# Local attention: the next row's preparation begins in the last step of the row ahead, turns of rotated rows stand later, output projections end blocks

## The chip, the cores and the metric

The kernel runs as one program on one core of a Trainium2 chip. The metric is the time of one launch on the device, in microseconds; the time of a kernel is the median of its runs. The engines are named as the profile names them: PE is TensorE (matrix products), PEld its weight loads, DVE is VectorE, ACT is ScalarE, POOL is GpSimd, SP is SyncE, which issues most transfers. Each engine takes its instructions from a queue of its own in a fixed order, and semaphores make it wait for the others.

## The reference, cut to what matters

The kernel computes a decoder of two layers on 8 rows of 512 tokens with 256 channels. The change lies in one part of it, the local attention, which occurs twice (once in each layer of a small local transformer). For each row it is:

```python
def _layer(x, wqkv, qs, ksc, wo, ...):
    h = shift_token(x)                 # half of the channels one token later
    qkv = h @ wqkv                     # 256 -> 3 * 512, 8 heads of 64
    q, k, v = jnp.split(qkv, 3, axis=-1)
    ...
    q = l2norm(q) * qs
    k = l2norm(k) * ksc
    q, k = rotary_xpos(q, k)           # cos, sin and a scale by position
    o = local_attention(q, k, v)       # windows of 128: own and previous one
    x = x + o @ wo                     # 512 -> 256
    ...                                # then a gated feed-forward on x
```

In `local_attention` a window of 128 queries sees the keys of its own window (causally) and of the one before; the softmax is over those.

## The kernel before, in words

The fast path (`FastDecoder`, `fast_stages`) runs self attention, cross attention, local attention 0, feed-forward 0, local attention 1, feed-forward 1, a quantized attention, a media attention and a mixture of experts. A stage is a Python generator that begins some of its work inside the stage ahead of it (`Ahead`); the local attention takes its row 0 through `prepare(0)` in that way.

**One row's preparation** (`prepare`, L1947) is cut into calls, which lie on eight slots of the row ahead of it:

- `turn(b, k)` (L1863): four transposes of the input's tiles into a bank, copied to `la_hT` by ScalarE.
- `project(b, i, j)` (L1882): tile i of 128 tokens (four tiles) times one third j of the weights: j = 0 and 1 are queries and keys, which ScalarE squares (`la_sq`, L1896) and copies (`la_qk`, L1897), j = 2 is the values, copied to `la_v` (L1894).
- `square` (L1901) and `root` (L1909): on VectorE, sums of squares by head and their inverse roots, for two tiles together.
- `rotate` (L1916): on VectorE, a scaling by the roots (L1920), two halves of the sine term (L1928, L1929), the cosine term (L1930) and an addition (L1931), on 128 x 1024 values.
- `turn_heads(b, i)` (L1933): eight transposes of the rotated tile in two banks of four, each copied to `la_qkT` by ScalarE (L1942).

**One row's attention** goes over four pairs of heads; a turn of the main loop (`for pair in range(0, n + 2, 2)`) takes one pair of heads and two slots. `scores(n)` (L1997) multiplies keys and queries into two PSUM tiles of two banks each, VectorE adds the mask (L2016) and ScalarE takes the exponential (L2020). `weigh(n)` (L2032) runs one pair later: values times weights into the bank `po`, copied to `la_o` by ScalarE (L2044); for each second pair also the denominators (`sum`), copied by VectorE (L2055). These go through DRAM (`inverted`, `times_rows`): two transfers, a reciprocal (L3306), one transfer, four broadcasts to `x_wide`, and then GpSimd multiplies (L3320) into `la_oT`. The last part is `project_out(b, i)` (L2067): four products for a tile of 128 tokens, added to the row by VectorE (L2076).

**Banks.** `turn`, `project`, `turn_heads` and `project_out` all take their PSUM bank from `self.pj()`, which has two buffers in turn. A group of products in a `pj` bank can start only when the reader of the group two before it is done.

**What sets the order.** The program's calls are laid out on the queues by a scheduler that takes priorities: what is made under `high_priority(self.AT_ONCE)` and in `together(n)` goes ahead, and `in_turn()` puts a call after the newest instruction of TensorE. `Background` (`later`) is a heap of calls with due times in ticks; each slot ticks it once and each call of a preparation once more. The output projections of a row come out of that heap, at 9, 12, 15 and 18 ticks after the last division:

```python
                    if c == 3:
                        for i in range(NST):
                            later.add(9 + 3 * i, lambda i=i: project_out(b, i))
```

The slots in the kernel before, with p = `project`, r = `rotate`, s = `square`, t = `turn_heads`: 0: both turns, p00, p01 and s0; 1: p10, p11, s1, root; 2: p20, r0, p21; 3: p30, r1, p31; 4: p02, s2, then t0, s3, root; 5: p12, r2, t1; 6: p22, r3, t2; 7: p32, t3.

Of the kernel before, what the change touches and what calls it, by code (L numbers as in the profile page):

```python
# [27 lines left out]
F32 = mybir.dt.float32  # L28
# [11 lines left out]
P = 128  # L40
# [1237 lines left out]
class FastDecoder(Decoder):  # L1278
# [557 lines left out]
    def local_attention(self, l, y, ahead):  # L1836
# [26 lines left out]
        def turn(b, k):  # L1863

            d = held.setdefault(b, {})
            if k == 0:
                d["hT"] = self.alloc(first, [P, 2, S], F32, "la_hT", bufs=1)
                d["v"] = self.alloc((first, second)[b % 2], [P, NST, S], F32, f"la_v{b % 2}", bufs=1)
                d["qkT"] = self.alloc((first, second)[b % 2], [P, 8, S], F32, f"la_qkT{b % 2}", bufs=1)
            hT = d["hT"]  # L1870
            ps = self.pj()
            for i in range(NST):
                nc.tensor.transpose(
                    ps[:, i * P : (i + 1) * P], y[:, b * NST + i, k * P : (k + 1) * P], self.ident
                )
            if k == 0:
                nc.scalar.copy(hT[:, 0, :], ps)
            else:
                nc.gpsimd.memset(hT[:, 1, 0:1], 0.0)
                nc.scalar.copy(hT[:, 1, 1:], ps[:, : S - 1])  # L1880

        def project(b, i, j):  # L1882
            d = held[b]
            if j == 0:
                d["rows", i] = self.alloc(first, [P, 2 * S], F32, "la_qk", bufs=4)
                d["sq"] = self.alloc(first, [P, 2 * S], F32, "la_sq")
            ps = self.pj()
            for k in range(2):
                nc.tensor.matmul(  # L1889
                    ps, d["hT"][:, k, i * P : (i + 1) * P], wqkv[:, k, j * S : (j + 1) * S],  # L1890
                    start=(k == 0), stop=(k == 1),
                )
            if j == 2:
                nc.scalar.copy(d["v"][:, i, :], ps)  # L1894
# [37 lines left out]

        def turn_heads(b, i):  # L1933
            d = held[b]
            for j in range(2):
                ps = self.pj()
                for c in range(4):
# [9 lines left out]
        def prepare(b):  # L1947

            def one(*calls):
# [8 lines left out]
                [one((p, 1, 0)), one((p, 1, 1), (s, 1), (root,))],  # L1958
                [one((p, 2, 0), (r, 0)), one((p, 2, 1))],
                [one((p, 3, 0), (r, 1)), one((p, 3, 1))],  # L1960
                [one((p, 0, 2), (s, 2)), one((t, 0), (s, 3), (root,))],
                [one((p, 1, 2), (r, 2)), one((t, 1))],
                [one((p, 2, 2), (r, 3)), one((t, 2))],
                [one((p, 3, 2)), one((t, 3))],
            ]

        second = None
# [7 lines left out]
        with self.tc.tile_pool(  # L1975
# [56 lines left out]
            def weigh(n):  # L2032
# [24 lines left out]
                def divide(rows):  # L2057
# [1 line left out]
                        oT = d["oT", c - 1 + j] = self.alloc(pool, [P, S], F32, "la_oT", bufs=6)  # L2059
                        self.times_rows(pool, oT, d["o", c - 1 + j], rows[2 * j : 2 * j + 2, :], later)  # L2060
                    if c == 3:
                        for i in range(NST):
                            later.add(9 + 3 * i, lambda i=i: project_out(b, i))

                self.inverted(pool, total[0:P:32, :], later, divide)

# [10 lines left out]

            n = 8 * B
            ahead.step()
            for pair in range(0, n + 2, 2):  # L2080
                if pair < n:
                    if pair % 8 == 0:
                        ready = prepare(pair // 8 + 1) if pair // 8 + 1 < B else [()] * 8
                    scores(pair // 2)
                if pair >= 2:
                    weigh(pair // 2 - 1)
                for i in (pair, pair + 1):
                    with self.in_turn():
                        later.tick(1)
                    if i < n:  # L2090
                        for thunk in ready[i % 8]:
                            with self.in_turn():
                                thunk()
                                later.tick(1)
                    if i == n - 6:
                        early.close()
                    if i > n - 6:
# [1 line left out]
                            ahead.step()  # L2099
            ahead.step(100)  # L2100
            later.drain()

    def local_ffn(self, l, y, ahead):

# [1472 lines left out]
```

## Time and profile before

| | us |
|---|---|
| median of 3 runs | 3036.18 (3035.45 to 3040.28) |
| the profiled execution, its own time | 3039.56 |
| its span, first to last instruction | 3037.8 |
| TensorE busy | 2832.6 |
| VectorE busy | 2039.3 |
| ScalarE busy | 1191.5 |
| GpSimd busy | 388.1 |
| local attention of layer 0, seven rows from 699.57 to 1087.59 | 388.0 |
| local attention of layer 1, seven rows from 1388.09 to 1773.18 | 385.1 |
| TensorE busy in these two stretches | 730.3 |

The page of the profile gives, for each group of instructions: the line of the kernel and the engine, what it writes and reads with the tiles' names, the number of instructions, their busy time and the mean of one in ns, and then the time that the engine sat idle just before them with the engine and line that ended it. A timeline gives the start and length of merged instructions, with the same idle time in brackets. The lengths of matrix products are modelled and overlap a little: a group that is followed at once by the next is listed some 0.15 us longer than the distance to the next start. The granted clock of TensorE over the whole execution is 0.972.

### The profile page before, as it was taken

To read this page: it belongs to the slowest core of one execution; us is meant where nothing else is said; L and a number is where in the kernel's file an instruction comes from. 1 tells how busy PE (TensorE), PEld (TensorE's weight loads), DVE (VectorE), ACT (ScalarE), POOL (GpSimd) and SP (SyncE) were. 2 spreads that over 40 slices of the span, in tenths; PEclk is the share of its full clock that TensorE was granted. 3 is DMA by queue.
4 is the path that set the end of the run, shared out by engine and by line. 5 is a ranking of instruction groups with operands and counts; after the bars stand their busy time and mean duration, and the time that the engine had idled before them with its cause. 6 is when DMAs were issued, how large, how long until landed. Compare 5 with 4: busy or idle time off the path is not lost. (4 is left out here: it accounts for less than half of the span.)

```text
span 3037.8 us, 39774 instructions
## 1 busy us (share of the span) xinstructions
PE 2832.6 (93%) x14929; PEld 1511.4 (50%) x14944; DVE 2039.3 (67%) x4546; ACT 1191.5 (39%) x1687; POOL 388.1 (13%) x357
## 2 busy tenths in 40 slices
PE   8999999979999999999999989998796999997998
PEld 5653333225555556555555556564444344444665
DVE  7458998977776784356776788548797766664110
ACT  2237776744444431124444431113364444441111
POOL 1111111100011110000101111101211012121111
PEclk9999999988999999999999999999897999997999
DMA  7011212101000011001000011001332132313331
GB/s 246 1 35 50 72 51 62 42 18 57 15 23 23 15 32 36 0 1 37 22 22 17 21 46 63 21 7 63 106 132 91 43 105 78 112 58 97 102 140 61
DMA packets 130694, 168.71 MB, mean 56 GB/s; under 512 B 51761, under 2 KB 79666, under 8 KB 128443
## 3 DMA queue, kind: packets, MB, share of 16 engines
q1 hardware_dynamic: 126394, 154.48, 16.3%
q0 software_dynamic: 4096, 11.59, 1.0%
q8 instruction: 119, 1.95, 0.3%
q14 instruction: 85, 0.69, 0.1%
HBM read 113.12 MB, written 47.50 MB: 53 GB/s over the span
## 5 line engine op out<-in xcount | busy, mean ns | idle before, releaser
L1889 PE MATMUL pj<-w,la_hT 128*128 128x512 f32 x720 | 334.2, 605 | 5.2 <-ACT la_qkT L1942 4.5
L1736 DVE TENSOR_TENSOR x_e<-x_e,x_share 128x1024 f32<-128x1024 f32 x256 | 315.9, 1277 | 14.3 <-ACT x_e L1735 14.1
L1735 ACT ACTIVATE x_e<-sc 128x1024 f32<-128x1024 f32 x256 | 249.2, 1023 | 83.8 <-PE sc L1724 83.8
L1889 PEld LDWEIGHTS pj<-w,la_hT 128*128 128x128 f32 x720 | 132.6, 191 | 153.4 <-issue 115.6
L2016 DVE TENSOR_TENSOR la_e<-sc,la_mask 128x1024 f32<-128x1024 f32 (+1 forms) x128 | 135.3, 1084 | 103.6 <-PE sc L2007 103.6
L3320 POOL TENSOR_TENSOR la_oT<-la_o,x_wide 128x512 f32<-128x512 f32 x64 | 97.7, 1538 | 753.1 <-DMA x_wide<-invs 678.6
L2945 ACT ACTIVATE ma_e<-sc,ma_bias 128x1024 f32<-128x1024 f32 x128 | 135.6, 1110 | 145.9 <-PE sc L2939 131.4
L2233 ACT ACTIVATE lf_gate<-pj,lf_b 128x512 f32<-128x512 f32 (+1 forms) x82 | 56.3, 687 | 333.3 <-PE pj L2212 318.0
L2020 ACT ACTIVATE la_e<-la_e 128x1024 f32<-128x1024 f32 (+1 forms) x128 | 117.5, 946 | 152.6 <-DVE la_e L2016 151.6
L2212 PE MATMUL pj<-lf_hnT,w 128*128 128x512 f32 (+1 forms) x368 | 171.4, 593 | 2.0 <-DVE lf_hid L2238 2.0
L1752 PE MATMUL po<-x_e,x_v 128*32 128x512 f32 x1024 | 140.7, 622 | 33.7 <-DVE x_e L1736 29.7
L2212 PE MATMUL sc<-lf_hnT,w 128*128 128x512 f32 x336 | 157.7, 592 | 0.0
L1724 PE MATMUL sc<-x_q,x_k 32*128 32x512 f32 x1024 | 152.9, 647 | 1.7 <-DVE sa_ok L1448 1.4
L2284 PE MATMUL po<-w,lf_hid 128*128 128x256 f32 x640 | 149.0, 379 | 0.0
L2238 DVE SCALAR_TENSOR_TENSOR lf_hid<-sc,lf_b,lf_gate 128x512 f32<-128x512 f32 x70 | 52.4, 749 | 136.4 <-PE sc L2212 133.4
L2027 PE MATMUL po<-la_e,la_v 128*64 128x256 f32 (+1 forms) x1024 | 125.8, 370 | 7.0 <-ACT la_o L2044 6.3
L2007 PE MATMUL sc<-la_qkT 64*128 64x256 f32 (+1 forms) x1024 | 128.9, 375 | 1.2 <-DVE la_e L2016 0.6
L2284 PEld LDWEIGHTS po<-w,lf_hid 128*128 128x128 f32 x640 | 117.8, 190 | 21.2 <-issue 7.4
L2939 PE MATMUL sc<-ma_qT,ma_kT 64*128 64x512 f32 x512 | 127.3, 615 | 0.4 <-ACT ma_e L2945 0.4
L2962 PE MATMUL po<-ma_e,ma_v 128*64 128x512 f32 x512 | 125.7, 612 | 0.0
L2070 PE MATMUL pj<-w,la_oT 128*128 128x256 f32 x512 | 121.0, 383 | 2.0 <-DVE lf_t L1480 0.7
L1905 DVE TENSOR_REDUCE la_ss<-la_sq 128x16 f32<-128x1024 f32 x64 | 77.7, 1215 | 65.8 <-ACT la_sq L1896 65.8
(500 smaller groups left out, 5173.6 us busy)
## 6 DMA issues: line engine op xcount, KB each, us to landing
x_wide<-invs SPq DMA_DIRECT2D x184, 128.0 KB
w<-in_f_w_dram SPq DMA_DIRECT2D x16, 1024.0 KB
kv<-kv_o SPq DMA_DIRECT2D x56, 256.0 KB
slots<-x_empty SPq DMA_DIRECT2D x8, 1028.0 KB
x_mask<-in_x_maskT_dram SPq DMA_DIRECT2D x8, 1024.0 KB
ma_kT<-kv SPq DMA_DIRECT2D x8, 1024.0 KB
ma_v<-kv SPq DMA_DIRECT2D x8, 1024.0 KB
ex_rows<-slots SPq DMA_DIRECT2D x7, 1028.0 KB
```

Of the source, the lines that this page charges most:

```text
L1724: nc.tensor.matmul(pair[r // 2][:, r % 2, :], d["k"][rows, g, kt * P : (kt + 1) * P], d["q"][rows, e, g, :], start=True, stop=True,)
L1735: nc.scalar.activation(ex, d["e"][rest][p], AF.Exp)
L1736: nc.vector.tensor_tensor(ex, ex, d["share"][:, kt, :].unsqueeze(1).broadcast_to([P, 2, 512]), ALU.mult)
L1752: nc.tensor.matmul(d["po"][32 * r : 32 * r + 32, :], d["v"][:, kt, 8 * g + 2 * r + e, :], ex[r // 2][:, r % 2, :], start=(kt == 0), stop=( ...
L1889: nc.tensor.matmul(ps, d["hT"][:, k, i * P : (i + 1) * P], wqkv[:, k, j * S : (j + 1) * S], start=(k == 0), stop=(k == 1),)
L2007: nc.tensor.matmul(both[half][:, r, jj * 256 : jj * 256 + to - j * P], d["qkT"][rows, 4 + c, j * P : (j + 1) * P], d["qkT"][rows, c, j * P ...
L2016: nc.vector.tensor_tensor(ex[:, :, :n_cols], ps[:, :, :n_cols], mask[:, :n_cols].unsqueeze(1).broadcast_to([P, 2, n_cols]), ALU.add,)
L2027: nc.tensor.matmul(out[:, j * P : to], lhsT(j), ex[:, jj * 256 : jj * 256 + to - j * P], start=(j == 0), stop=(j == 3), skip_group_check=True,
L2212: nc.tensor.matmul(ps[:m, :], w1[:, k, at : at + m], held[b]["hnT"][:, k, :], start=(k == 0), stop=(k == 1))
L2284: nc.tensor.matmul(ps[:, :C], held[b]["hid"][:, f, i * P : (i + 1) * P], w2[:, f, :], start=(f == 0), stop=False,)
L2939: nc.tensor.matmul(both[m // 2][:, r, :], d["k"][rows, c, kt * P : (kt + 1) * P], d["q"][rows, c, :], start=True, stop=True,)
L2945: nc.scalar.activation(ex, ps, AF.Exp, bias=bias[:, b * NST + kt : b * NST + kt + 1], scale=0.125)
```

## The change

Three things are moved in `local_attention`; the instructions of a row stay the same.

The preparation has nine lists in place of eight, and the first of them (both turns of the input, p00, p01, s0) is placed at the end of slot 7 of the row two before, so it lies behind t2 and t3 of the row one before. The others move up by one slot. The slots are now: 0: p10, p11, s1, root; 1: p20, r0, p21; 2: p30, r1, p31; 3: p02, s2, s3, root; 4: t0, p12, r2; 5: t1, p22, r3; 6: p32; 7: t2, t3, and then the first list of the next row. For row 1 the first list is put at the head of slot 0.

The output projections are no longer taken from the heap at fixed ticks. Two ticks after the last division they join a list `due`, and the end of each turn of the main loop takes from it 0, 1, 1 or 2 tiles by the pair's number; what is left is done after the stage.

The buffers of the values and of the turned heads are allocated at their first use rather than with the turned input.

```diff
@@ turn
             if k == 0:
                 d["hT"] = self.alloc(first, [P, 2, S], F32, "la_hT", bufs=1)
-                d["v"] = self.alloc((first, second)[b % 2], [P, NST, S], F32, f"la_v{b % 2}", bufs=1)
-                d["qkT"] = self.alloc((first, second)[b % 2], [P, 8, S], F32, f"la_qkT{b % 2}", bufs=1)
@@ project
             if j == 2:
+                if i == 0:
+                    d["v"] = self.alloc((first, second)[b % 2], [P, NST, S], F32, f"la_v{b % 2}", bufs=1)
                 nc.scalar.copy(d["v"][:, i, :], ps)
@@ turn_heads
+            if i == 0:
+                d["qkT"] = self.alloc((first, second)[b % 2], [P, 8, S], F32, f"la_qkT{b % 2}", bufs=1)
@@ prepare
                 [one((p, 1, 0)), one((p, 1, 1), (s, 1), (root,))],
                 [one((p, 2, 0), (r, 0)), one((p, 2, 1))],
                 [one((p, 3, 0), (r, 1)), one((p, 3, 1))],
-                [one((p, 0, 2), (s, 2)), one((t, 0), (s, 3), (root,))],
-                [one((p, 1, 2), (r, 2)), one((t, 1))],
-                [one((p, 2, 2), (r, 3)), one((t, 2))],
-                [one((p, 3, 2)), one((t, 3))],
+                [one((p, 0, 2), (s, 2), (s, 3), (root,))],
+                [one((t, 0)), one((p, 1, 2), (r, 2))],
+                [one((t, 1)), one((p, 2, 2), (r, 3))],
+                [one((p, 3, 2))],
+                [one((t, 2)), one((t, 3))],
@@ divide
                     if c == 3:
-                        for i in range(NST):
-                            later.add(9 + 3 * i, lambda i=i: project_out(b, i))
+                        later.add(2, lambda: due.extend((b, i) for i in range(NST)))
@@ main loop
+            due = []
+            coming = prepare(1)
+            first_calls = coming[0]
             for pair in range(0, n + 2, 2):
                 if pair < n:
                     if pair % 8 == 0:
-                        ready = prepare(pair // 8 + 1) if pair // 8 + 1 < B else [()] * 8
+                        b = pair // 8
+                        ready = list(coming[1:]) if b + 1 < B else [()] * 8
+                        coming = prepare(b + 2) if b + 2 < B else [()] * 9
+                        ready[7] = [*ready[7], *coming[0]]
+                        if b == 0:
+                            ready[0] = [*first_calls, *ready[0]]
...
+                for tile in due[: (0, 1, 1, 2)[pair // 2 % 4]]:
+                    with self.in_turn():
+                        project_out(*tile)
+                    due.remove(tile)
...
             later.drain()
+            for tile in due:
+                project_out(*tile)
```

More of the change, by code (lines that the diff above doesn't have):

```diff
@@ L2094, in local_attention @@
                                 later.tick(1)
+                for tile in due[: (0, 1, 1, 2)[pair // 2 % 4]]:
+                    with self.in_turn():
+                        project_out(*tile)
+                    due.remove(tile)
+                for i in (pair, pair + 1):
                     if i == n - 6:
```

## The prediction

> **What bounds the kernel now.** I read the busy table first, then the groups of instructions, then the stage itself as a timeline of each engine. The busy table says TensorE: 2832.6 us of 3037.8.
>
> ```profile
> PE 2832.6 (93%) x14929; PEld 1511.4 (50%) x14944; DVE 2039.3 (67%) x4546; ACT 1191.5 (39%) x1687; POOL 388.1 (13%) x357
> ```
>
> So only what TensorE waits for can be won. In the groups, one line of the two local-attention stages stands out:
>
> ```profile
> L1939 PE MATMUL pj<-ident,la_qk 128*128 128x128 f32 x480 | 77.6, 285 | 40.4 <-DVE x L2076 31.5 <-ACT la_qkT L1942 6.3 <-ACT la_v L1894 2.0
> ```
>
> The turns of rotated rows wait 40.4 us in all, 31.5 of it for the VectorE addition that empties an output projection's bank. One row of the first stage, on TensorE, shows where:
>
> ```profile
> 887.24 1.72 PE L2027 MATMUL sum<-la_e,ones 128*32 128x256 f32 x32
> 888.89 1.99 PE L2070 MATMUL pj<-w,la_oT 128*128 128x256 f32 x8
> 890.72 1.88 PE L1889 MATMUL pj<-w,la_hT 128*128 128x512 f32 x4
> 893.37 0.66 PE L1939 MATMUL pj<-ident,la_qk 128*128 128x128 f32 x4 [0.77 <-DVE x L2076]
> 893.95 1.79 PE L2007 MATMUL sc<-la_qkT 64*128 64x256 f32 x16
> 895.67 0.66 PE L1939 MATMUL pj<-ident,la_qk 128*128 128x128 f32 x4
> 896.16 1.89 PE L2070 MATMUL pj<-w,la_oT 128*128 128x256 f32 x8
> 897.89 1.88 PE L1889 MATMUL pj<-w,la_hT 128*128 128x512 f32 x4
> 900.82 0.66 PE L1939 MATMUL pj<-ident,la_qk 128*128 128x128 f32 x4 [1.05 <-DVE x L2076]
> ```
>
> Two banks named pj alternate over turns, projections and outputs, so each group waits for the reader of the group two before it. Here output, projection, turn: the turn needs the output's addition (0.33 us), which stands in VectorE's queue behind parts of a rotation of 1.2 us each. The third wait of the row is 0.70. Over the ten rows after the first two of each stage these three sum to 2.82 us a row on average (2.28 to 3.38), of some 55.4. [...] ScalarE's queue is in order, and what stands in it matters below:
>
> ```profile
> 899.00 1.79 ACT L2020 ACTIVATE la_e<-la_e 128x1024 f32<-128x1024 f32 x2 [2.05 <-DVE la_e L2016]
> 900.70 0.57 ACT L1894 COPY la_v<-pj 128x512 f32<-128x512 f32 x1
> ```
>
> The two exponentials wait for VectorE's mask additions, and the copy that frees a pj bank waits behind them. And a long wait has an aftermath; the turn that waits 2.79 is followed by weighing at 2.88 instead of 1.73, the one that waits 2.19 is not:
>
> ```profile
> 734.76 0.66 PE L1939 MATMUL pj<-ident,la_qk 128*128 128x128 f32 x4 [2.79 <-ACT la_qkT L1942]
> 735.35 2.88 PE L2027 MATMUL po<-la_e,la_v 128*64 128x256 f32 x16
> ...
> 1422.51 0.65 PE L1939 MATMUL pj<-ident,la_qk 128*128 128x128 f32 x4 [2.19 <-ACT la_qkT L1942]
> 1423.10 1.73 PE L2027 MATMUL po<-la_e,la_v 128*64 128x256 f32 x16
> ```
>
> **The change, part by part.** Nothing is added or taken away: per row 8 query/key projections, 4 value projections, 8 half turns, 4 outputs, 14 DMAs on SP. All is order. The built order of a middle row, counted from T, the end of the last denominators of the row before (865.16 in the row above), is now: half a turn of the input, projections 0 and 1 of tile 0, outputs 2 and 3, tiles 1 and 2, scores of pair 1, weighing, tile 3, value 0, output 0, scores 2, weighing, sums, turn 0 (two halves), scores 3, value 1, turn 1a, weighing, turn 1b, values 2, output 1, value 3, turns 2 and 3.
>
> *Taken away:* the three waits, 3.3 us a row. Outputs 2 and 3 stand at T+4 to T+7.5, where VectorE has only a reduction and a reciprocal ahead of their additions: the first is done at T+6.6, and tile 1 needs its bank at T+7.5. Output 0 has scores, weighing, sums and a half turn (5.5 us) between it and the group that needs its bank. No wait.
>
> *Put in its place, first: value 0.* From the row at 865 (start to start): projection 1.77, value 1.72, output 1.73, scores 1.71, weighing 1.67, sums 1.65, half turn 0.53. TensorE ends tile 1 at T+11.05, tile 2 at 14.6, scores 16.3, weighing 18.0, tile 3 at 21.5. VectorE starts the second reduction at 11.9 (1.13), then the root (2.72), two scalings (2.28), then the masks of pair 1 (2.0): 20.0. In ScalarE's order both exponentials (second one: 0.25 after its mask, 0.75), a copy of la_o (0.5), and only then square and copy of tile 3 (1.0): 22.5. Value 0 needs that bank: wait 1.0. In the kernel before, pair 1's masks came ahead of the reductions, so nothing waited here. GpSimd's two products lie over the root as before, where every other row lost 0.7 (turn 0 waits 0.77 in some rows, about 1.6 in others): +0.4 on average.
>
> *Second: turn 1b.* VectorE has no gap from T+20.0: two sine halves 1.20, reduction 1.13, cosine and addition 2.26, reduction 1.13, sine halves 1.20, output addition 0.33, cosine 1.13, 0.2, mask 1.0, addition 1.13, mask 1.0, rest of the root and the sums' copy 2.85, two scalings 2.28, masks of pair 3 2.0. Sum 18.9: T+38.9. Exponential, 0.25 later, 0.75; copy of value 1, 0.5; TensorE 0.14 later: 40.5. TensorE itself arrives: value 0 at 22.6, then 1.72+1.73+1.71+1.67+1.65+1.06+1.71+1.72+0.53+1.67 = 15.2: 37.8. Wait 2.7; a trace would show about 2.4 to 2.5[...]. Before, one scaling fewer stood ahead of these masks, and they ended at T+34.6.
>
> *Third:* turn 2 waits for output 1's addition (T+46.3) with TensorE there at 46.2: 0.2. The first projection waits 0.2 for its turned input, whose scores no longer stand between; the scores after turn 2 keep their 0.4 to 0.6.
>
> Per row: 1.0 + 0.4 + 2.7 + 0.2 + 0.2 = 4.5 against 3.3 and 0.3 of the interleaved scores' last wait, which goes: **+0.9**. Ten middle rows: +9.0. The first two rows of a stage, walked alike: the first waits at a turn as long as before (2.79 and 2.19 in the two stages), the second 2.1 at turn 1b where it had 1.6 to 1.7 twice with less after it; I take +0.3 a stage, +0.6.
>
> *The clock.* In this trace waits of 2.71, 2.79, 2.82 and 2.84 us were followed by matmuls at nearly double time, waits of 2.19 and 2.60 were not. One drop costs what the rows at 735 to 741 show: 1.14 on the weighing and 0.45 on the half turn, about 1.6. [...] By the rows it stands 0.25 short of the shortest wait that did[...]: ten rows, one drop taken, +1.6, bounds 0 and 10 x 1.6 = 16. I go by the rows: **+11.2**.
>
> *Edits at nothing.* The reciprocal of pairs 0 and 1 moves from T+36.1 to T+39.9; its DMAs and GpSimd's products follow 5.3 later (T+45.2). The la_o of pair 3 reuses pair 0's buffer (three buffers) and is copied at T+51.5, after the first product's end at 46.7: cover 5 us. The products now lie over the last rotation ahead of output 1's addition. The row for it: an addition of 1.22 took 1.97 at 907.73, with GpSimd busy. TensorE, already 2.7 late, has 0.6 to spare, so +0.1. [...] The later allocation of values and turned heads frees nothing that was waited for (value 0's buffer was last read before T). SP's queue keeps its order and count. The eight outputs of the last two rows stay behind the feed-forward's first chunk; the preparation of row 0 keeps its 18 calls. Nothing.
>
> Sum: 3039.56 (the profiled execution, span 3037.8) + 11.2; the median of the runs is 3.4 lower, 3036.18, so **3047**.
>
> **The rivals.** (a) *Faster:* turn 1b's wait is covered. It decides where pair 3's masks end: by T+36.3 instead of 38.9. Then value 1 is copied when TensorE arrives, the three old waits go (10 x 3.3), 1.4 + 0.4 stay: -1.8 x 10 = -18, 3018. For it: ScalarE is only 39% busy. Against: VectorE's 18.9 us hold no gap. (b) *No change:* turn 1b's wait is 1.8 us, as with VectorE 3% quicker than walked: +0 to +3, 3037. (c) *Clock in every row:* the wait crosses 2.7 in each: +9.6 + 16 to 28 (the drop at 1788.48 cost 2.8), 3062 to 3074.
>
> **How the numbers follow.** Likeliest, new waits with at most a few drops: 0.55 (3042.5 to 3054). (c) 0.15, (b) 0.18, (a) 0.12. The bound of 0.2% (6 us) is about what a measurement of this kernel can tell. Slower takes the likeliest case and (c), less a little of its lower edge: 0.69; same 0.19; faster 0.12. The range leaves half of (a) and half of (c) out: 3030 to 3065.
>
> **What would show it.** Right: turns no longer wait for the addition of x (31.5 us before); a half turn waits about 2.4 us for ScalarE's la_v in each middle row, value projections about 1 us for la_qk; TensorE's busy time unchanged; rows of about 56.3 us. Wrong: a half-turn wait under 1.5 us (VectorE's queue shorter than walked), or weighings of 2.9 us in each row (the clock).

## The result and the profile after

The changed kernel takes 3057.61 us (median of four runs, 3056.47 to 3061.03), the kernel before 3036.61 us beside it: 1.0071 times as long, 95% interval 1.0057 to 1.0085. The forecast was 3047. Its profiled span is 3059.3 us against 3037.8, so there are 21.5 us to find, where the sum had 11.2.

Two lines of the page and of the groups answer to those shown of before: TensorE's busy time, and the turns, with the projections beside them.

```profile
PE 2842.1 (93%) x14944; PEld 1518.6 (50%) x14944; DVE 2028.2 (66%) x4546; ACT 1184.8 (39%) x1687; POOL 383.5 (13%) x357
```

```profile
L1887 PE MATMUL pj<-w,la_hT 128*128 128x512 f32 x720 | 341.3, 614 | 19.5 <-ACT la_qk L1897 16.7 <-ACT la_qkT L1944 1.5 <-ACT la_hT L1875 0.7
L1941 PE MATMUL pj<-ident,la_qk 128*128 128x128 f32 x480 | 74.1, 288 | 40.1 <-ACT la_v L1894 31.7 <-DVE x L2078 5.8 <-ACT la_qkT L1944 2.0
```

The turns wait as long as before (40.1 against 40.4 us), but for somebody else: 31.7 us for ScalarE's copy of values where 31.5 us were for the addition of x. New are 16.7 us of the projections (5.2 in all before). TensorE is busy 9.5 us longer with the same products (15 of them, none in these stages, have no record in the trace of before); the projections alone went from 334.2 to 341.3. A row of the first stage, on TensorE, shows the new waits in their places:

```profile
883.16 3.70 PE L1887 MATMUL pj<-w,la_hT 128*128 128x512 f32 x8
888.55 1.98 PE L1887 MATMUL pj<-w,la_hT 128*128 128x512 f32 x4 [1.69 <-ACT la_qk L1897]
...
902.31 1.73 PE L2030 MATMUL po<-la_e,la_v 128*64 128x256 f32 x16
906.30 0.66 PE L1941 MATMUL pj<-ident,la_qk 128*128 128x128 f32 x4 [2.25 <-ACT la_v L1894]
...
910.33 1.88 PE L1887 MATMUL pj<-w,la_hT 128*128 128x512 f32 x4
912.76 0.66 PE L1941 MATMUL pj<-ident,la_qk 128*128 128x128 f32 x4 [0.55 <-DVE x L2078]
```

Value 0 waits 1.69 us for tile 3's copies, the second half turn of tile 1 waits 2.25 us, the turn of tile 2 waits 0.55. ScalarE's queue answers for the second in the same way as before:

```profile
903.99 1.79 ACT L2023 ACTIVATE la_e<-la_e 128x1024 f32<-128x1024 f32 x2 [4.31 <-DVE la_e L2019]
905.68 0.56 ACT L1894 COPY la_v<-pj 128x512 f32<-128x512 f32 x1
```

All this is as forecast. What the forecast walked, but didn't read as a limit of its own, is VectorE's timeline in that row. These are its first instruction behind a gap, the one after it, the masks of pair 3, the last two, and the next behind a gap:

```profile
877.08 1.22 DVE L1905 TENSOR_REDUCE la_ss<-la_sq 128x16 f32<-128x1024 f32 x1 [3.64 <-ACT la_sq L1896]
878.34 1.11 DVE L1913 TENSOR_SCALAR la_ss<-la_ss 128x32 f32<-128x32 f32 x1
...
902.74 2.08 DVE L2019 TENSOR_TENSOR la_e<-sc,la_mask 128x1024 f32<-128x1024 f32 x2
...
911.15 1.23 DVE L1931 TENSOR_TENSOR la_qk<-la_qk,la_r 128x1024 f32<-128x1024 f32 x1
912.30 0.41 DVE L2078 TENSOR_TENSOR x<-x,pj 128x256 f32<-128x256 f32 x1
914.84 1.23 DVE L2019 TENSOR_TENSOR la_e<-sc,la_mask 128x1024 f32<-128x1024 f32 x1 [2.14 <-PE sc L2010]
```

VectorE never stops from the squares of tile 1 to the addition that lets the turn of tile 2 begin: 35.6 us of a row of 57.9. In the kernel before the same stretch is there, with fewer instructions in it:

```profile
875.87 1.22 DVE L1905 TENSOR_REDUCE la_ss<-la_sq 128x16 f32<-128x1024 f32 x1 [2.38 <-ACT la_sq L1896]
877.12 0.43 DVE L1913 TENSOR_SCALAR la_ss<-la_ss 128x32 f32<-128x32 f32 x1
...
907.40 0.41 DVE L2076 TENSOR_TENSOR x<-x,pj 128x256 f32<-128x256 f32 x1
```

So a row can be read in another way, with T the end of the last denominators of the row before. Before: the stretch starts at T + 10.7, takes 31.9 us, and from the turn of tile 2 to the row's end TensorE needs 12.5: 55.1. After: it starts at T + 11.8, since two outputs stand ahead of tile 1, takes 35.6, and 10.45 follow: 57.9. Of the 3.7 us more, 3.5 are found: the masks of one pair of heads more (2.0), one last addition of a rotation more (1.15), 0.7 on a small instruction beside GpSimd's products (1.11 against 0.43), one output addition less (0.33). Two readings of one row, then: waits on TensorE that add up, or VectorE's stretch. The experiments tell them apart.

**The ledger of the 21.5 us**, from the starts and ends of rows in the two traces:

| stretch | before | after | difference |
|---|---|---|---|
| start of stage 0 (first scores) | 698.13 | 696.00 | -2.1 |
| first scores to the end of row 2, both stages | 111.2 + 108.5 | 108.2 + 101.8 | -9.7 |
| rows 3 to 6, eight in all | 222.4 + 221.6 | 235.3 + 232.2 | +23.5 |
| rows 7 and 8, both stages | 75.8 + 76.2 | 82.4 + 81.9 | +12.3 |
| end of stage 0 to start of stage 1 | 280.5 | 276.7 | -3.9 |
| behind stage 1 | 1243.3 | 1244.8 | +1.5 |

A middle row is 55.5 us before and 58.4 after. The first two rows end sooner and the last two later in part because work has changed places: in each stage row 2 holds two output projections where it held four, and row 7 six. Two of them take 3.5 us of TensorE.

### The profile page after: what moved, and what is told of

Read it like the earlier page. It is cut to its first block, busy times and chain, and to the rows that moved or that the text cites. A ratio compares the mean times of both kernels' runs of the same rounds, so it can differ in the third digit from the quotient of the medians.

```text
span 3059.3 us, 39825 instructions
## 1 busy us (share of the span) xinstructions
PE 2842.1 (93%) x14944; PEld 1518.6 (50%) x14944; DVE 2028.2 (66%) x4546; ACT 1184.8 (39%) x1687; POOL 383.5 (13%) x357
## 3 DMA queue, kind: packets, MB, share of 16 engines
q1 hardware_dynamic: 126394, 154.48, 16.2%
## 5 line engine op out<-in xcount | busy, mean ns | idle before, releaser
L1887 PE MATMUL pj<-w,la_hT 128*128 128x512 f32 x720 | 341.3, 614 | 19.5 <-ACT la_qk L1897 16.7
L2010 PEld LDWEIGHTS sc<-la_qkT 64*128 64x128 f32 x1024 | 93.8, 187 | 49.9 <-issue 20.4
```

What stands on the lines that cost most here:

```text
L1887: nc.tensor.matmul(ps, d["hT"][:, k, i * P : (i + 1) * P], wqkv[:, k, j * S : (j + 1) * S], start=(k == 0), stop=(k == 1),)
L2010: nc.tensor.matmul(both[half][:, r, jj * 256 : jj * 256 + to - j * P], d["qkT"][rows, 4 + c, j * P : (j + 1) * P], d["qkT"][rows, c, j * P ...
```

## The experiments

The theories: **1**, the recorded one, sums the waits on TensorE, so a wait that is taken away is paid back. **2**: VectorE's stretch sets when the turns of tiles 2 and 3 can come, and a wait ahead of them on TensorE only hides it. **3**: the clock, lowered behind waits. Each ratio is to the kernel before, run beside it on the same chip (3035.2 to 3039.4 us on the three chips of the experiments). The middle row is the mean of rows 3 to 6 of both stages, taken from each trace. The last column is the mean of those of the eight in which the profile shows a granted clock of 1.00 throughout, with their number: it leaves out what theory 3 is about.

| kernel | median us | ratio, 95% interval | middle row, us | at full clock, us (rows) |
|---|---|---|---|---|
| before | 3036.61 | 1 | 55.51 | 55.51 (8) |
| changed | 3057.61 | 1.0071 (1.0057 to 1.0085) | 58.44 | 57.84 (5) |
| changed, ScalarE's order | 3068.76 | 1.0100 (1.0078 to 1.0122) | 59.24 | 58.19 (3) |
| changed, VectorE's order | 3055.04 | 1.0052 (1.0032 to 1.0071) | 58.35 | 57.19 (2) |
| changed, both orders | 3034.11 | 0.9988 (0.9974 to 1.0003) | 55.96 | 55.96 (8) |
| changed, counts 2, 1, 1, 0 | 3054.59 | 1.0051 (1.0036 to 1.0065) | 58.26 | 57.56 (4) |
| counts, ScalarE's order | 3031.84 | 0.9984 (0.9975 to 0.9993) | 55.71 | 55.70 (8) |
| counts, both orders | 3025.10 | 0.9955 (0.9945 to 0.9965) | 55.35 | 55.35 (8) |
| counts, both orders, pair 1 | 3032.60 | 0.9985 (0.9976 to 0.9994) | 55.60 | 55.60 (8) |
| the same, output of block 1 held ahead | 3036.30 | 0.9993 (0.9983 to 1.0003) | 56.50 | 55.80 (3) |
| before, outputs at block ends | 3031.15 | 0.9971 (0.9960 to 0.9983) | 55.28 | 55.28 (8) |
| the same, ScalarE's order | 3037.99 | 1.0008 (0.9995 to 1.0022) | 55.61 | 55.08 (6) |
| changed without new grouping | 3044.11 | 1.0018 (1.0006 to 1.0031) | 56.54 | 56.54 (8) |
| changed without outputs at block ends | 3062.67 | 1.0078 (1.0052 to 1.0104) | 58.83 | 58.78 (5) |

### One order on ScalarE, one on VectorE, and both

The exponentials of pair 3 go behind the copy of value projection 1. TensorE, VectorE and GpSimd keep their orders.

```diff
-                nc.scalar.copy(d["v"][:, i, :], ps)
+                copied = nc.scalar.copy(d["v"][:, i, :], ps)
+                if i == 1:
+                    d["v1"] = copied.ins
...
-                    nc.scalar.activation(ex[:, :, :n_cols], ex[:, :, :n_cols], AF.Exp, scale=-1.0)
+                    with self.tc.issue_after(held[b + 1]["v1"]) if c == 3 and b + 1 < B else nullcontext():
+                        nc.scalar.activation(ex[:, :, :n_cols], ex[:, :, :n_cols], AF.Exp, scale=-1.0)
```

> The changed kernel with one order turned round on ScalarE: in each of the 14 rows that prepare another, the two exponentials of head pair 3 are issued behind the copy of the value projection of tile 1 instead of ahead of it (TensorE, VectorE and GpSimd keep their orders). Theory 1, the recorded one: the half turn of tile 1 waits 2.25 us for that copy and this wait is paid in full, so the kernel loses about 14 x 2.2 = 31 us: about 3027 us, and the half turn of tile 1 doesn't wait. Theory 2, VectorE's stretch: from the square reduction of tile 1 (877.08 in the row that starts at 865.29) to the addition ahead of the turn of tile 2 (912.71) VectorE has no gap, 35.6 us, and the wait at tile 1 only hides that the turn of tile 2 would come no sooner. Then the wait at tile 1 goes and the wait of the turn of tile 2 for the addition of x grows from 0.55 to about 2.8 us; the time stays within 4 us of 3057.6. Theory 3, the clock: the waits of 2.25 us lower the granted clock and cost by that; then about 7 us are gained, since projections took 341.3 us against 334.2 before.

Measured: 3068.76 us, slower than the changed kernel. TensorE in this kernel, in the same place of the same row:

```profile
899.51 1.73 PE L2033 MATMUL po<-la_e,la_v 128*64 128x256 f32 x16
901.17 0.66 PE L1943 MATMUL pj<-ident,la_qk 128*128 128x128 f32 x4
...
905.33 1.88 PE L1887 MATMUL pj<-w,la_hT 128*128 128x512 f32 x4
909.96 0.66 PE L1943 MATMUL pj<-ident,la_qk 128*128 128x128 f32 x4 [2.75 <-DVE x L2081]
```

The half turn of tile 1 (901.17) no longer waits. The turn of tile 2 does, 2.75 us for VectorE's addition instead of 0.55: the 2.25 us came back 5.9 us of work later, to within 0.05. Theory 1 falls here. Theory 2 has the wait right but not the time: the row of this excerpt is 57.9 us long, as in the changed kernel, others are up to 60.5. The idle time ahead of the local groups (the turns of the input left out) is the same in both profiles (71.7 and 71.2 us), while TensorE's busy time in them is 865.5 against 858.9. So part of what it lost, by the rows 0.45 of 0.80 us, is products run at a lower clock, in theory 3's way, behind the one wait of 2.75: in five of the eight middle rows the granted clock is 0.94 to 0.97, and these take 59.1 to 60.5 us; the other three take 57.9 to 58.6.

Next the other order alone: the addition that frees the bank goes ahead of the end of tile 3's rotation (ScalarE's order is that of the changed kernel).

```diff
-            nc.vector.tensor_tensor(q4, q4, cos, ALU.mult)
-            nc.vector.tensor_tensor(qk, qk, r, ALU.add)
+            if i == 3:
+                d["last"] = (qk, q4, cos, r)
+            else:
+                end_rotate(qk, q4, cos, r)
...
+        def end_last(b):
+            if adds:
+                with self.tc.issue_after(adds[-1]):
+                    end_rotate(*held[b]["last"])
+            else:
+                end_rotate(*held[b]["last"])
...
-                [one((p, 3, 2))],
+                [one((end_last,), (p, 3, 2))],
...
-                    nc.vector.tensor_tensor(yt, yt, ps[:, :C], ALU.add)
+                    adds.append(nc.vector.tensor_tensor(yt, yt, ps[:, :C], ALU.add).ins)
```

> The changed kernel with one order turned round on VectorE: the addition of the output projection that frees the bank for the turn of tile 2 goes ahead of the last two multiplications and additions of tile 3's rotation instead of behind them. ScalarE's order is that of the changed kernel. Both theory 1 and theory 2 expect only the 0.55 us that the turn of tile 2 waits: 14 x 0.55 = 8 us at most, about 3050 us, since the half turn of tile 1 still waits 2.25 us for ScalarE. VectorE now waits up to 0.6 us for the output projection itself.

Measured: 3055.04 us. As both theories had it, little: the half turn of tile 1 still waits for ScalarE (30.8 us in all), and the intervals of this kernel and the changed one overlap.

Then both together:

> Both orders turned round at once, ScalarE's (exponentials of pair 3 behind the copy of value projection 1) and VectorE's (the addition ahead of the end of tile 3's rotation). Theory 1: what the first alone gives, 31 us, and the 8 us of the second: about 3019 us. Theory 2: neither wait holds now, and the next that does is the turn of tile 3 behind its rotation, 2.0 to 2.3 us a row sooner than in the changed kernel: 14 x 2.1 = 29 us, about 3028 us; decisive is that the two together give three to four times the sum of what each gives alone.

Measured: 3034.11 us, no longer to be told from the kernel before. In units of the kernel before the two orders give +0.29% (a loss) and -0.19% alone, and -0.83% together, 25 us. The rows at full clock say the same without the clock: 57.84 us in the changed kernel, 58.19 and 57.19 with one order, 55.96 with both. TensorE's waits in the first stage, by what they wait for (total, times, longest):

```profile
PE pj L1888 <- ACT la_qk L1900: 8.5, 5, 2.2
PE pj L1957 <- DVE la_qk L1940: 6.5, 5, 2.9
...
PE pj L1957 <- DVE x L2095: 2.3, 6, 1.1
```

This is theory 2's forecast (3028) with the 29 us a little too large: behind the two waits stands a third, the turn of tile 3 for its rotation, 0.9 us in four of the eight middle rows.

### More slack for VectorE

The outputs at the ends of blocks in the counts 2, 1, 1, 0: the two that stood between tile 0 and tile 1 come behind tile 2.

```diff
-                for tile in due[: (0, 1, 1, 2)[pair // 2 % 4]]:
+                for tile in due[: (2, 1, 1, 0)[pair // 2 % 4]]:
```

> The changed kernel with the output projections at block ends in the counts 2, 1, 1, 0 instead of 0, 1, 1, 2: the two that stood between the projections of tile 0 and of tile 1 (869.36 to 872.82 in the row that starts at 865.29) come behind the projections of tile 2. Theory 2: VectorE's stretch starts with tile 1's squares, so it starts about 3.5 us sooner in each row and holds two additions (0.33 us each) more: a row shrinks by up to 2.8 us, until the TensorE's own work of 53.4 us and what waits are left bind; 14 x 2 to 2.8 = 28 to 39 us, 3019 to 3030 us. Theory 1: the two waits for ScalarE stand behind exponentials, whose scores come no sooner, so they stay (1.4 to 2.3 and 2.25 us): within 5 us of 3057.6.

Measured: 3054.59 us, middle rows 58.26: theory 1's number. The stretch did start 3.5 us sooner in the row (T + 8.3), as theory 2 had it, but little came of it (0.3 us a row at full clock). VectorE's end of the stretch, and TensorE at tile 1:

```profile
907.63 1.23 DVE L1931 TENSOR_TENSOR la_qk<-la_qk,la_r 128x1024 f32<-128x1024 f32 x1
909.60 0.42 DVE L2078 TENSOR_TENSOR x<-x,pj 128x256 f32<-128x256 f32 x1 [0.74 <-PE pj L2072]
```

```profile
905.37 0.65 PE L1941 MATMUL pj<-ident,la_qk 128*128 128x128 f32 x4 [2.51 <-ACT la_v L1894]
```

Now VectorE waits 0.74 us for TensorE, and TensorE 2.51 us for ScalarE. In the changed kernel the two limits lay within 0.55 us of each other; either alone holds the row. That corrects theory 2: not VectorE alone, but the later of two paths, through the masks to ScalarE's copy and through the rotations to the addition. It says that with VectorE's slack the same edit on ScalarE should pay at last. That was run with both orders first:

> The changed kernel with three edits: output projections at block ends in the counts 2, 1, 1, 0; the exponentials of pair 3 behind the copy of value projection 1; the addition ahead of the end of tile 3's rotation. With the counts alone the row took 57.56 us, VectorE's stretch began 3.4 us sooner in the row and ended in an idle 0.74 us, so VectorE no longer held the turn of tile 2; the half turn of tile 1 still waited 2.51 us for ScalarE. Theory 2 (two engines in turn: the wait that is removed only counts when the other engine has slack): now there is slack, and the 7 waits of a stage (16.9 us) are paid back in full: 2 x 17 = 34 us below the 3054.6 us of the counts alone, about 3020 us; the half turn of tile 1 and the turn of tile 2 wait under 0.5 us. If VectorE still bound the row, it would stay near the 3034 us of the two orders without the counts.

Measured: 3025.10 us, 0.45% faster than the kernel before (0.35 to 0.55), and the fastest of all; theory 2 had 3020. And with ScalarE's order alone on top of the counts:

> The changed kernel with the counts 2, 1, 1, 0 and the exponentials of pair 3 behind the copy of value projection 1, but with VectorE's addition where the changed kernel has it, behind the end of tile 3's rotation: it differs from the kernel with the counts alone (3054.6 us) in ScalarE's order alone, and from the kernel with three edits (3025.1 us) in VectorE's order alone. Theory 1: the 2.51 us a row are paid back, 34 us: 3021 us. Theory 2: the rotation of tile 3 ends 44.9 us into the row and the addition behind it at 45.2, so the turn of tile 2, which TensorE would reach 43.5 us into the row, waits about 1.7 us and 0.8 us of the 2.5 us are gained: 11 us, about 3043 us, and 18 us more by moving the addition.

Measured: 3031.84 us. Between this kernel and the one with the counts alone only ScalarE's queue differs, and it is 0.67% faster, 20 us; without the counts the same edit cost 9. At full clock a middle row falls from 57.56 to 55.70 us, 1.9 of the 2.51 that the wait held. The forecast of 3043 was too slow: it had TensorE at the turn of tile 2 at T + 43.5, but in this trace the turn starts at T + 45.3, behind a wait of 0.17 us instead of the 1.7 expected.

```profile
906.44 0.66 PE L1943 MATMUL pj<-ident,la_qk 128*128 128x128 f32 x4 [0.17 <-DVE x L2081]
```

The addition's place is worth the rest, 0.29% or 9 us, between this and the kernel with three edits.

### The wait of value projection 0

In the kernel with three edits one wait over 0.2 us is left in a middle row, 1.79 us of value projection 0 for tile 3's copies, which stand behind the exponentials of pair 1:

```profile
934.85 1.98 PE L1888 MATMUL pj<-w,la_hT 128*128 128x512 f32 x4 [1.79 <-ACT la_qk L1900]
...
952.85 1.99 PE L2089 MATMUL pj<-w,la_oT 128*128 128x256 f32 x8 [0.19 <-ACT la_qkT L1960]
```

A fourth edit issues these behind the copies of tile 3's first projection.

```diff
+                    one_exp = lambda e=ex[:, :, :n_cols]: nc.scalar.activation(e, e, AF.Exp, scale=-1.0)
+                    if c == 1 and b + 1 < B:
+                        late.append(one_exp)
+                        continue
...
                                 thunk()
+                                if i % 8 == 2 and late:
+                                    with self.tc.issue_after(self.newest(mybir.EngineType.Activation)):
+                                        while late:
+                                            late.pop(0)()
```

> The three edits, and a fourth: the exponentials of pair 1 are issued behind the squares and copies of tile 3's first projection, which stood behind them, so that the value projection of tile 0 finds its bank free. It waits 1.4 to 2.2 us in five rows of a stage in every kernel so far (8.5 to 9.0 us a stage). VectorE's stretch (T + 8.4 to T + 45.3) and the 8 us of TensorE's work behind the turn of tile 3 leave a row of 53.3 us, as long as TensorE's own 53.4 us. Theory 2: 2 x 9 = 18 us below the kernel with three edits, about 3003 us. If VectorE binds sooner than that sum says, the turn of tile 3 waits for its rotation, and under 8 us are gained.

Measured: 3032.60 us, 7 us slower than without it. Value projection 0 waits no more, and two others do. TensorE:

```profile
887.35 0.66 PE L1957 MATMUL pj<-ident,la_qk 128*128 128x128 f32 x4 [0.90 <-DVE x L2099]
...
897.24 1.99 PE L2093 MATMUL pj<-w,la_oT 128*128 128x256 f32 x8 [1.20 <-ACT la_qkT L1960]
```

0.90 + 1.20 stand for 1.79 + 0.19, and the row goes from 55.35 to 55.60. That is 2.0 us over the eight middle rows, of 6.0 between the two traces; 3.4 more lie behind the second stage, outside the local attention, and aren't explained here. The edit had also let the scheduler put pair 2's scores and masks ahead of the output that ends block 1 and its addition. The next kernel holds them behind it:

```diff
-                    with self.tc.high_priority(self.AT_ONCE):
+                    with self.tc.high_priority(self.AT_ONCE), (
+                        self.tc.issue_after(adds[-1]) if c == 2 and adds else nullcontext()
+                    ):
...
-                    scores(pair // 2)
+                    with self.in_turn() if pair % 8 == 4 else nullcontext():
+                        scores(pair // 2)
```

> The kernel with four edits (3032.6 us) with one more: scores of pair 2 are issued behind the output projection that ends block 1, and their masks behind its addition, as they were with three edits (3025.1 us). With four edits the wait of value projection 0 (1.79 us a row) was gone, but the turn of tile 0 waited 0.90 us for that addition and an output projection 1.20 us for ScalarE. Theory 2: the 0.90 us go, the 1.20 us stay, since they hang on the masks of pair 3: 55.6 - 0.9 = 54.7 us a row, 10 to 13 us less, about 3020 us. If the turn waits for something else by then, 3030 us or more.

Measured: 3036.30 us; the miss that its last sentence names. Now the scores of pair 3 wait for VectorE's masks of pair 2, which empty their bank. Two rows of this kernel on TensorE:

```profile
892.48 2.04 PE L2026 MATMUL sc<-la_qkT 64*128 64x256 f32 x16 [2.07 <-DVE la_e L2037]
894.78 3.22 PE L1888 MATMUL pj<-w,la_hT 128*128 128x512 f32 x4 [0.26 <-ACT la_qkT L1960]
...
949.62 1.79 PE L2026 MATMUL sc<-la_qkT 64*128 64x256 f32 x16 [2.07 <-DVE la_e L2037]
951.92 1.98 PE L1888 MATMUL pj<-w,la_hT 128*128 128x512 f32 x4 [0.51 <-ACT la_qkT L1960]
```

In all five kernels with both orders or the counts and ScalarE's order, 2.0 to 2.4 us of waits a row stay. That VectorE's work as such sets 55.3 us isn't shown by this: no kernel here took work off it. The two rows also show the clock: the same wait of 2.07 us is followed by products at their usual time (1.98) in one and at 3.22 in the other, where the granted clock is 0.50 from 893.88 on; rows of the two kinds are 55.8 and 56.9 to 57.2 us long.

### The parts of the change alone

The third part alone, on the kernel before:

> The kernel before with the third part of the change alone: its output projections at block ends in the counts 0, 1, 1, 2; preparation as before, all eight steps within the row. In the kernel before, turns wait 31.5 us for the addition of x. Theory 1 (waits on TensorE's list add up): most of them go and nothing takes their place: 3010 to 3020 us. Theory 2 (VectorE's stretch sets the turns): VectorE has the same work between tile 1's squares and the turns, less an addition or two (0.33 us each) and the masks of one pair that stand ahead of the stretch now; but two outputs stand ahead of the tile projections and start the stretch later; 3030 to 3045 us.

```diff
-                        for i in range(NST):
-                            later.add(9 + 3 * i, lambda i=i: project_out(b, i))
+                        later.add(2, lambda: due.extend((b, i) for i in range(NST)))
...
+                for tile in due[: (0, 1, 1, 2)[pair // 2 % 4]]:
+                    with self.in_turn():
+                        project_out(*tile)
+                    due.remove(tile)
```

Measured: 3031.15 us, 0.29% faster than the kernel before and in theory 2's range. No turn waits for the addition of x any more, and still most of the 31.5 us are not won: 23.9 us are now for ScalarE's copy of a half turn and 8.3 for the rotation itself.

```profile
L1939 PE MATMUL pj<-ident,la_qk 128*128 128x128 f32 x480 | 74.5, 283 | 34.4 <-ACT la_qkT L1942 23.9 <-DVE la_qk L1931 8.3 <-ACT la_v L1894 2.0
```

The first two parts without the third:

> The changed kernel without its third part: the early first step and the later turns stay, output projections are added as ticks 9, 12, 15, 18 as in the kernel before. Theory 1: the waits for the copy of value projection 1 (31.7 us) and for tile 3's copies (16.7 us) hang on the first two parts and stay, and additions stand ahead of turns again: 3057 to 3070 us. Theory 2: one output instead of two stands ahead of tile 1's projections, so VectorE's stretch starts 1.7 us sooner and holds one or two more additions (0.33 us each): 1 us a row less, 3040 to 3050 us.

```diff
-                        later.add(2, lambda: due.extend((b, i) for i in range(NST)))
+                        for i in range(NST):
+                            later.add(9 + 3 * i, lambda i=i: project_out(b, i))
...
-                for tile in due[: (0, 1, 1, 2)[pair // 2 % 4]]:
-                    with self.in_turn():
-                        project_out(*tile)
-                    due.remove(tile)
```

Measured: 3062.67 us. Here theory 1's number held and theory 2's did not: the waits for ScalarE stayed (32.3 and 16.2 us), and turns waited 10.5 us for additions. In the row that starts at 864.91 the stretch starts 1.9 us sooner than in the changed kernel, but it lasts 0.7 longer, and the output projection that no longer stands ahead of tile 1 stands behind the turn of tile 2, where TensorE needs 12.2 us to the row's end instead of 10.45: 58.4 us in all. Theory 2's forecast had left that output out.

The first and third without the second, the grouping of turns, values and rotations:

> The changed kernel without its second part: the first step of preparation starts in the row ahead and output projections end blocks, but turns, values and rotations are grouped as in the kernel before, all one slot sooner, with nothing but the next row's first step in slot 7. If the loss comes from the regrouping (turns two steps later, behind the exponentials of pair 3), this is at 3020 to 3037 us; if it comes from the early first step with the two outputs between tile 0's and tile 1's projections, which start VectorE's stretch later, it is at 3050 us or more.

```diff
-                [one((p, 0, 2), (s, 2), (s, 3), (root,))],
-                [one((t, 0)), one((p, 1, 2), (r, 2))],
-                [one((t, 1)), one((p, 2, 2), (r, 3))],
-                [one((p, 3, 2))],
-                [one((t, 2)), one((t, 3))],
+                [one((p, 0, 2), (s, 2)), one((t, 0), (s, 3), (root,))],
+                [one((p, 1, 2), (r, 2)), one((t, 1))],
+                [one((p, 2, 2), (r, 3)), one((t, 2))],
+                [one((p, 3, 2)), one((t, 3))],
+                [],
```

Measured: 3044.11 us, between the two cases. In units of the kernel before: outputs at block ends -0.29%; the early first step on top of them +0.47%; the new grouping on top of both +0.53%. Both parts cost, each about 15 us. The outputs' part gains 9 alone; beside the others it gains 2, which the intervals don't tell from nothing.

### The same test on another kernel

In the kernel with the outputs at block ends the second half turn of tile 0 waits behind the exponentials of pair 3. One order turned round there, as in the first experiment:

```diff
-                nc.scalar.copy(
+                copied = nc.scalar.copy(
...
+                if i == 0:
+                    d["t0"] = copied.ins
...
+                    with self.tc.issue_after(held[b + 1]["t0"]) if c == 3 and b + 1 < B else nullcontext():
```

> The kernel before with its output projections at block ends (3031.2 us) and one order turned round on ScalarE: the exponentials of pair 3 behind the copy of the second half turn of tile 0, which now waits behind the first of them (1.47 us a row, 23.9 us in all, longest 2.78 us). The other engines keep their orders. Theory 1: these 20 us or so are gained: about 3011 us. Theory 2: VectorE runs from tile 1's squares to the end of tile 2's rotation without a gap (927.13 to 955.62), so the next turn, which waits 0.81 us for that rotation, waits about 2.2 us instead: 3027 to 3035 us, or some us more where the longer wait lowers the clock.

Measured: 3037.99 us, 0.37% slower where theory 1 had it 20 us faster. The waits for ScalarE's copy fell from 23.9 to 1.4 us, those for the rotation rose from 8.3 to 29.1. The clearest place:

```profile
957.71 1.58 PE L1939 MATMUL pj<-ident,la_qk 128*128 128x128 f32 x8 [2.48 <-DVE la_qk L1931]
```

Its products take 1.58 us, 1.09 elsewhere: here the wait costs clock. Two of the eight middle rows run at a granted clock of 0.97; the other six take 55.08 us, 0.2 less than without the edit. So at full clock the order gives next to nothing, as theory 2 had it, and with the clock the mean row is 0.3 us longer.

## Why the prediction was right in sign and half in size

**Right.** The new waits stand where they were put, and for the reason given. Turn 1b: "about 2.4 to 2.5" in the trace, 2.25 measured. Turns waiting for the addition of x: 31.5 us went to 5.8. Value 0: 1.0 + 0.4 expected, 16.7 us in ten middle rows, 1.67 each. The rotation that now lies under GpSimd's products: 0.1 a row expected; its last addition takes 1.23 us in nine of the ten rows and 2.34 in one. Together with the turn of tile 2 (0.2 expected; 5.8 us over nine waits, 0.6) a middle row's waits are about 4.5 us. The working's 3.3 and 4.5 count with each wait the 0.16 us by which a group that is followed at once runs into the next (in the kernel before, the outputs at 888.89 are listed at 1.99 us, and the next group starts 1.83 later; 3.3 is 2.82 and three times 0.16). The measured 4.5 are without it, so the walk was short by some 0.5 us.

**Wrong, the row's sum.** "4.5 against 3.3 and 0.3" gave +0.9 a row, 7.2 us for the eight rows of the ledger. They came to 23.5, 2.9 a row: 1.6 from waits (4.47 against 2.83 as the trace shows them, where the working had 4.5 - 3.3 = 1.2), 0.7 from TensorE's own work, and 0.5 from the clock. The step "and 0.3 of the interleaved scores' last wait, which goes", and with it the statement that TensorE's busy time stays, failed with the opposite sign. In the two rows compared above TensorE's starts without waits add up to 52.69 us before and 53.43 after; the eight middle rows of before all lie at 52.6 to 52.7, and the five at full clock after at 53.42. By kind, the denominators take 3.84 and 4.40, the scores 7.57 and 7.97, the other products 0.2 less in sum. The end of a row shows why, before and after:

```profile
917.76 1.05 PE L2027 MATMUL sum<-la_e,ones 128*32 128x256 f32 x10
918.74 0.49 PE L2007 MATMUL sc<-la_qkT 64*128 64x128 f32 x4
919.16 1.28 PE L2027 MATMUL sum<-la_e,ones 128*32 128x256 f32 x22
```

```profile
919.64 0.63 PE L2030 MATMUL sum<-la_e,ones 128*32 128x256 f32 x4
920.20 0.48 PE L2010 MATMUL sc<-la_qkT 64*128 64x128 f32 x2
920.61 0.62 PE L2030 MATMUL sum<-la_e,ones 128*32 128x256 f32 x2
921.16 0.48 PE L2010 MATMUL sc<-la_qkT 64*128 64x128 f32 x2
921.57 1.70 PE L2030 MATMUL sum<-la_e,ones 128*32 128x256 f32 x26
```

Scores cut the denominators into three groups instead of two. Two products of 128 x 256 between scores take 0.55 us from start to start, where 26 in a row take 1.64. In this end of a row TensorE changes between the two four times instead of twice; why a short group takes so long was not shown. The term is +0.74 us a row against -0.3: about 1.0 of the 2.0 us by which a row was forecast too short, and the largest single miss.

**Wrong, the clock's size.** One drop of 1.6 us for ten rows was put on top of 9.6 (9.0 and 0.6), since a wait of 2.45 us stood 0.25 short of the shortest with a drop behind it, 2.71. Three of the eight middle rows ran at a granted clock of 0.97, and without their waits they take 54.8 to 55.0 us, 1.4 to 1.6 more than the 53.42 of the other five: 4.3 us. Behind the half turn of 906.30 nothing slowed; a row later, behind the same wait, it did:

```profile
964.01 1.12 PE L1941 MATMUL pj<-ident,la_qk 128*128 128x128 f32 x4 [2.26 <-ACT la_v L1894]
964.92 3.14 PE L1887 MATMUL pj<-w,la_hT 128*128 128x512 f32 x4
```

The granted clock tells these two waits apart. In each trace it falls to 0.50 for 3.41 us or a whole multiple of that (the last time until the trace ends), and all these falls come whole multiples of 3.41 us apart. On this grid a boundary cuts the first wait; the second lies within one stretch, and the half clock begins at that stretch's end:

| stretch of the grid, us | of the wait in it | TensorE busy | granted clock |
|---|---|---|---|
| 902.59 to 906.00 | 1.96 | 1.46 | 1.00 |
| 906.00 to 909.42 | 0.30 | 3.12 | 1.00 |
| 960.62 to 964.03 | 2.26 | 1.15 | 1.00 |
| 964.03 to 967.44 | 0 | 3.41 | 0.50 |

The 14 traces hold 151 waits of over 1.7 us in rows 1 to 7. Of the 47 with 1.97 us or more in one stretch of the grid, 46 were followed by the half clock at its end; of the other 104, 3 were. So the 2.7 us that the prediction drew from the trace of before are no bound: what parts equal waits in these traces is how much of them falls into one stretch, and waits of 2.25 to 2.26 us in the changed kernel went either way. It doesn't account for all of them: one of the three drops, at 854.80, came behind a wait of 1.67 us.

**Wrong, how a wait is priced.** Rival (a) said that a covered turn 1b would pay back its wait and give 3018. The first experiment covered it, by ScalarE's order and not by earlier masks, and the time rose to 3069. "VectorE's 18.9 us hold no gap" stood in the working, but only as what delays the masks; that the same queue holds the addition for the next turn 6.5 us later, so that the wait has a second owner, was not followed. Rival (b), no change, is excluded by the interval; (c), a drop in every row, was too strong: it happened in three of eight, and 3057.6 lies below its 3062.

**The ends of the stage.** The first two rows of a stage were put at +0.6 in all; they gained 9.7 us, while the last two, one of them a middle row of the prediction, lost 12.3. The two output projections that went from row 2 to row 7, which the prediction didn't count there, are 6.9 us of either figure and cancel. All that lies outside the ledger's eight rows came to -2.0 us, where the sum had 4.0. That hides part of the miss in the middle.

## What to carry to other kernels

Before a wait is priced at its length, follow the other engines' queues to the next thing the waiting engine needs: if a second queue runs without a gap to within a fraction of a microsecond of that point (0.55 us here), the wait is not for sale alone. Test it by turning one order round and looking whether the same microseconds appear at the next wait; where two limits lie side by side, edits pay only together (+9 and -6 us alone, -25 together), and giving one engine slack first changes what the next edit is worth (from +9 to -20 us). Compare rows at full clock first: behind the same wait of 2.07 us the next products took 1.98 us in one row and 3.22 in another. When work is regrouped, count also how it cuts other groups on the main engine.

## What the runs showed that was not expected

- A lower clock behind waits well under 2.7 us: 1.97 and 2.26 us in the changed kernel, 2.07 in the kernel with five edits, and not behind equal waits in other rows. It came in 46 of the 47 cases in which 1.97 us or more of the wait lay within one stretch of a fixed grid of 3.41 us, and in 3 of the other 104. In the kernels with three and four edits, whose middle rows hold no wait over 1.8 us, all eight of those rows are within 0.1 us of each other.
- Denominators cut into groups of two by scores cost 0.55 us a group. What this time consists of was not measured.
- A VectorE instruction on 128 x 32 values took 1.11 us where it met GpSimd's two products, and 0.17 at 894.53, where it met none. The long one started at 878.34, 0.20 behind the start of the second product, and ended at 879.45, 0.04 behind its end.
